# A cross-attention and MLP block on one Trainium2 core: in the last five of 32 attention units the ones product runs on the sum of the two key halves, under a newly planned order

## The chip, the cores and the metric

The kernel runs on one core of a Trainium2 chip. The core's engines are TensorE (PE, matrix products; PEld is its weight load), VectorE (DVE), ScalarE (ACT), GpSimd (POOL) and SyncE (SP), which here issues the DMA transfers. The engines run side by side and meet at semaphores. The metric is the time of one execution on the device in microseconds (us). The kernel before took 677.11, 676.02 and 676.46 us in three runs, median 676.46.

## The reference

One transformer block in fp32: layer norm, cross-attention with 16 heads, residual, layer norm, MLP with gelu, residual. There are 8 batches of 256 tokens, the width D is 512, the MLP's 2048, a head has 32 columns, and the context has 256 keys per batch. The mask is all ones.

```python
x = layer_norm(hidden_states, ln1_w, ln1_b)
q = (x @ q_w + q_b)...                       # to (B, 16 heads, 256, 32)
k = (encoder_hidden_states @ k_w + k_b)...
v = (encoder_hidden_states @ v_w + v_b)...
scores = jnp.einsum('bhqd,bhkd->bhqk', q, k) * scale
scores = jnp.where(mask, scores, mask_value)
attn = jax.nn.softmax(scores, axis=-1)
out = jnp.einsum('bhqk,bhkd->bhqd', attn, v)
hidden = out @ cproj_w + cproj_b + residual  # out as (B, 256, 512)
y = layer_norm(hidden, ln2_w, ln2_b)
y = jax.nn.gelu(y @ fc_w + fc_b, approximate=True)
return hidden + y @ proj_w + proj_b
```

## The kernel before, in words

The tokens are worked on in two groups of 1024 (g = 0 and 1, four batches each). Every large matrix product is done by a recursion with seven products instead of eight (`quad`, line 837): products P1 to P7 go to PSUM banks, and DVE, ACT or POOL add them up (operations named t1 to t3 and c11 to c22) and make the sums of the operands beforehand (`sums`, line 816; names such as x1t1 for sums of activations, and pw1s1 or pw1i2_4 for sums of weights). The MLP's two products, fc and pd, do this on two levels (`grown`, line 1146).

**Attention** is cut into 32 units, 16 for each group. A unit is named by three digits: group, head group (four heads) and batch; unit 123 is group 1, head group 2, batch 3. For each unit `scores` (line 991) and `attend` (line 1039) record these operations, named by kind and unit:

- `s` on PE: the scores of four heads, keys on the partitions, in two halves of 128 keys; eight matmuls in row shape.
- `ev` on ACT (eight): copies from PSUM to the two tiles `pr`, with the mask's bias.
- `mx` (two), `mt` on DVE, `mc` (three) on ACT, `fold` on DVE: the maxima over the keys for each query. Then `md` stores them to DRAM and `mm` loads them back on all partitions; both are issued by SP.
- `less` (two, on POOL or DVE): subtract the maxima. `exp` (two) on ACT.
- `av` on PE, in column shape: eight matmuls with a matrix of ones give the sums over the keys (four heads, two halves of the keys each, added up in PSUM), and eight with the values give the output. A matmul of fp32 shows as two records in the profile.
- `r` on DVE (maximum over equal rows with a transpose, reciprocal, transpose), and `att` on DVE (output times reciprocal).

The code knows a second kind of unit. A string of letters, one for each unit of a group in order of work, chooses it (line 502); all 32 are `p` before. For a unit with the letter `z`, `scores` also records two additions `ss` of 128x512 (one for each `pr` tile, on DVE or POOL) that add the two halves of the keys, and `attend` issues four matmuls with ones on that sum instead of eight on the halves:

```python
if ss:
    sums_ = [(lambda j=j: tile_of(av)[j * HD : (j + 1) * HD, 256:512], lambda: ones, lambda j=j: at(ss, j), True) for j in range(4)]
else:
    sums_ = [(lambda j=j: tile_of(av)[j * HD : (j + 1) * HD, 256:512], lambda: ones,
              lambda j=j, kc=kc: at(pt[j // 2], 2 * (j % 2) + kc), kc == 0) for kc in range(2) for j in range(4)]
```

The units of a group go in the order of `units_of` (line 1321); the last five of group 1 are 123, 111, 131, 113 and 133.

**The order is written out by hand.** The kernel first records all 2,927 operations (class `Order`, line 44), each with the buffers that it reads and writes. `run` (line 94) then reads a long string, `PROGRAM` (line 124), in which each operation stands once, and plays it back: `name:V`, `:A` or `:G` puts it on DVE, ACT or POOL, and a name without a letter goes to its usual engine. A second string, `PLACES`, gives each buffer its slot of SBUF (45 slots of 128x1024 and smaller ones) or its bank of PSUM (three for the projections, five for scores and outputs). So the order in which an engine runs its instructions is the order of the words, and an instruction that waits holds up all that stands behind it on its engine. All DMA is issued by SP in this order too, so a load that stands behind a store that waits is late with it.

Around unit 003, one of group 0's last, the words in `PROGRAM` (lines 186 to 196) run, on PE: s003, av001, v1_1_P7, three turns (transposes), av032, q1_0_P1, s023, v1_1_P4, a turn, v1_0_P4, s011, q1_1_P1, av021, s031, av003. The keys of unit 011 come from DRAM by the load ku011, which stands far ahead (line 164). Between fold003 and less003_0 DVE has pw1s3, pw1i6_3, less021, pw1i6_1, less021 again, att032, mx023 twice, mt023, pw1i6_4 and x1t1; pw1i7_1 stands between the two less003.

Behind the last unit of group 0, av033, PE has s120, o0_0_P2, o0_0_P1, o0_1_P1, s110 and o0_0_P6 (the o products are the attention's output projection). o0_0_P6 needs a0t2, a sum of attention outputs on DVE, and this needs r033, att033 and a copy on ACT, ab0_111. While units of group 1 go through their softmax, PE runs fc products of group 0.

Of the kernel before, what the change touches and what calls it, by code (L numbers as in the profile page):

```python
# [124 lines left out]
cq0_00_0 cq0_00_1 vw00 rows8 kw00 cq0_01_1 mk rows4 turn_c0_10 cq0_01_0 turn_c0_00 c0_10:V cq0_11_0 c0_00:A  # L125
cq0_11_1 rows6 small k0_0_P1 kw11 cq0_10_0 rows2 k0_1_P1 kw10 cq0_10_1 rows3 turn_c0_11 rows1 turn_c0_01 c0_11:A
turn_c0_21 fw0_00_0 c0_01:V turn_c0_31 vw11 c0_21:V v0_1_P1 c0_31:A rows5 c0t3:V kw01 xt0_0 v0_0_P1 kws1:G rows7
rows0 vw10 kws3:V turn_c0_20 fw0_10_0 mk~1 turn_c0_30 c0t1:V c0_20:A k0_1_P7 vw01 c0_30:A fw0_11_1 v0_0_t1:A
v0_1_t1:V kws2:G fw0_11_0 k0_0_P2 fw0_10_1 c0t2:V fw1_11_1 fw0_00_1 kws4:G cols k0_1_P2 cols~1 fw0_01_1 k0_1_t1:A
vws1:V xt0_2 k0_0_t1:A vws3:G xt0_7 k0_1_P6 k0_1_c11 xt0_3 xt0_1 c0t4:V fw1_10_1 k0_0_P6 xt0_5 vws2:V xt0_4 fw0s1:V  # L130
xt0_6 v0_1_P6 k0_0_t2:A fw0s2:V fcd0_5_False k0_1_t2:A qw00 vws4:V k0_1_P5 fw0_01_0 v0_1_t2:A stats_x0_10 fw0i6_3:G
xt1_2 fw0s3:V v0_1_P5 stats_x0_00 fw1i4_1:G stats_x0_11 fw0i5_3:G v0_0_P6 k0_0_c11 fw0i1_1:G stats_x0_21 aggr_x0_11
fw0i2_1:V aggr_x0_10 v0_1_P2 fw0i1_2:V fw0i7_1:V stats_x0_01 fw0i1_4:G aggr_x0_21 fw0i1_3:V k0_0_P5 aggr_x0_01
fw0i7_2:G aggr_x0_00 fcd0_1_True eps_x0_0 fw1_01_0 fw0i6_1:V pow_x0_0 v0_0_t2:V fw1_01_1 v0_0_P2 v0_1_t3:V
fw0i7_3:G k0_0_t3:A xt1_0 stats_x0_20 fw1_11_0 eps_x0_1 aggr_x0_20 eps_x0_2 fw0i5_1:V fcd0_7_False v0_0_P5 pow_x0_1
stats_x0_30 fw0i2_3:V stats_x0_31 fw0i6_2:G nb_x0_1 v0_1_P3 pow_x0_2 aggr_x0_30 norm_x0_11:A fw1_00_1 nb_x0_0
aggr_x0_31 fw0i5_2:G norm_x0_10:A qw10 nb_x0_2 qw11 fw1i2_1:V k0_1_t3:A k0_0_P3 fw0i2_2:V fw1_10_0 v0_0_t3:A
fw1i4_2:V k0_1_c22 fw0i2_4:G norm_x0_01:A fcd0_6_False eps_x0_3 fw1_00_0 fw1i4_3:V norm_x0_20:A k0_1_P3 pow_x0_3
v0_1_c11 norm_x0_00:A fw0i6_4:V v0_0_c11 fw0i7_4:G v0_0_P3 fw1i4_4:V fcd0_7_True fw0i5_4:G qw01 qws1:V fcd0_5_True
nb_x0_3 turn_x0_30 norm_x0_31:V fcd1_4_True k0_0_c12:A turn_x0_10 qws2:V turn_x0_00 x0_10:A fw1i2_3:V turn_x0_20  # L140
x0_00:A k0_1_P4 qws3:V v0_0_c12:A fw1i1_3:V x0_30:A fw1s1:V q0_0_P1 norm_x0_30:A fw0s4:V fcd1_5_False norm_x0_21:A
vd0_0_11 x0_20:A fw1s2:V turn_x0_21 fcd0_2_True k0_1_c12:A turn_x0_01 fcd0_6_True turn_x0_31 fw1i1_1:V kd0_0_11
turn_x0_11 fw1i5_1:V xt1_3 q0_1_P1 fw1s3:V v0_1_c12:A x0_21:A x0_01:V fw1i5_2:G x0_31:A q0_0_P2 fw1i1_2:G q0_0_t1:V
x0_11:A k0_1_c21 fw1i1_4:G q0_1_t1:A q0_1_P2 q0_0_c11 pw0_00_11 fw1i2_2:V x0t1:V fcd1_6_False kd0_1_12 s000
fcd1_7_False x0t2:V pw0_00_10 k0_0_P7 ev000_00 x0t3:V stats_x1_00 ev000_21 q0_0_P6 ev000_30 fw1i5_3:V ev000_31
aggr_x1_00 fw1s4:V q0_1_P6 q0_0_t2:A fw1i2_4:V x0t4:V ev000_10 fcd1_2_True q0_0_P5 fw1i5_4:V q0_1_t2:A stats_x1_10
fw1i7_3:G fcd1_5_True ev000_01 k0_0_c22 fcd0_3_False ev000_11 qws4:G stats_x1_11 fcd1_1_True q0_0_P7 q0_0_t3:A
fcd1_3_False mx000_0 fw1i3_1:G ev000_20 pw0_00_00 fw1i3_3:G ct1_4 k0_0_P4 q0_0_c22 ct1_1 fw0i3_3:G ct1_0 fw0i3_1:V
ct1_3 mx000_1 fw1i7_1:G q0_0_P4 fw0i4_3:G q0_1_P7 q0_0_c21 aggr_x1_10 q0_1_c11 k0_0_c21 q0_1_P5 aggr_x1_11
fw0i3_2:V mt000 fw0i3_4:V mc000_2 fw1i6_1:V mc000_3 fcd0_3_True mc000_1 fw1i3_2:V s020 q0_1_t3:A fw1i6_2:V fold000  # L150
fw1i3_4:G q0_1_c22 q0_0_P3 md000 fw1i6_3:G ev020_01 ev020_30 fcd1_3_True eps_x1_1 ev020_10 pow_x1_1 ct1_7 ev020_31
# [8 lines left out]
mc022_2 av000 ev010_01 ev010_21 less020_0:V ev010_10 ev010_30 ev010_00 k1_1_P1 exp020_1 c1t1:V mm002 ev010_20  # L160
fold022 ev010_11 c1t2:G exp020_0 k1_0_P1 mx010_0 md022 pw0_10_01 ev010_31 r000 q0_1_c12:A av020 k1_1_t1:A pw0i1_4:G
att000 k1_0_t1:A mx010_1 c1t3:G prd0_1_True mm022 s030 mt010 r020 mc010_2 mc010_3 mc010_1 k1_0_P6 ev030_21 fold010
ev030_11 pw0_01_11 less002_1:V ev030_00 md010 ev030_01 ev030_10 xt1_1 k1_1_P6 ev030_20 k1_0_t2:V pw0_10_10 ev030_30
less002_0:V ev030_31 pw0_01_00 exp002_1 pw0_10_00 k1_0_P5 less022_1:G mx030_0 ku011 exp002_0 pw0_01_10 mm010
# [318 lines left out]
def pool(n):  # L483
# [17 lines left out]
}  # L501
KINDS = ("pppppppppppppppp", "pppppppppppppppp")


SERVE = {
# [964 lines left out]
```

## Time and profile before

| | |
|---|---|
| median of three runs | 676.46 us (676.02 to 677.11) |
| profiled execution | 676.35 us |
| its span | 674.6 us |
| granted clock of TensorE, mean | 0.997 |
| instructions | 11,523 |
| busy: PE, PEld | 98%, 74% |
| busy: DVE, ACT, POOL | 86%, 50%, 56% |

The profile is of one execution. Its page has a line with the busy time of each engine, the span in 40 slices (each digit is the busy share in tenths; PEclk is the clock that TensorE was granted, in tenths), the chain of work that ended last, and groups of instructions (line, engine, operation, output<-inputs, shape, count, busy time and mean length in ns). The trace behind it answers with the waits (who waited for whom: us in total, times, longest), windows (busy time of each engine in a stretch) and a timeline (start, length, engine, line, operation). Names there are by kind of buffer: a row `av<-pr,ones` is a product with ones of some unit, and one finds which by the order of the words. Some buffers are shared: a name such as `vws` can stand for values of a unit.

### The profile page before, as it was taken

The page shows a single profiled execution, that of the slowest core. Times are in us where ns is not written, and L with a number is a line of the kernel's source. Part 1 is how long each engine was busy: PE and PEld are TensorE (multiplying, and loading weights), DVE is VectorE, ACT ScalarE, POOL GpSimd, SP SyncE. Part 2 cuts the span into 40 slices and gives each one's busy share as a digit, 9 for nine tenths or more (in the row PEclk, how much of TensorE's full clock was granted, in tenths as well). Part 3 has the DMA queues.
Part 4 walks back from the last instruction along what each step waited for, and adds up shares of the span by engine and source line. Part 5 has one row for each costly group of instructions (what it writes and reads, how often), then busy time and mean ns, then how long its engine had stood idle before and what let it go on. Part 6 is the DMA issues. An engine that isn't in the chain of part 4 may idle for free.

```text
span 674.6 us, 11523 instructions
## 1 busy us (share of the span) xinstructions
PE 663.8 (98%) x4001; PEld 498.3 (74%) x4001; DVE 578.3 (86%) x969; ACT 340.1 (50%) x699; POOL 379.1 (56%) x340
## 2 busy tenths in 40 slices
PE   9999999999899999999999999999999999999997
PEld 7674564478544676777687888888888888888886
DVE  2889889999999999999889999998489877896874
ACT  1246488768999979976764872001040221930000
POOL 1552556575578999977945743310636247518542
PEclk9999999999989999999999999999999999999999
DMA  8989888987957635445552646997999586842686
GB/s 264 329 273 337 306 286 257 295 258 211 307 164 241 210 113 203 157 142 170 174 190 95 220 130 167 267 245 250 165 243 237 133 243 149 232 144 57 192 166 118
DMA packets 173034, 140.65 MB, mean 209 GB/s; under 512 B 83712, under 2 KB 133424, under 8 KB 172976
## 3 DMA queue, kind: packets, MB, share of 16 engines
q1 hardware_dynamic: 172976, 139.92, 70.5%
q8 instruction: 32, 0.52, 0.3%
q14 instruction: 26, 0.21, 0.1%
HBM read 102.00 MB, written 37.88 MB: 207 GB/s over the span
## 4 chain that ended last, share of the span: by engine, by line
PE 92%; DVE 4%; DMA 3%; ACT 1%; issue 0%; SPq 0%; POOL 0%; DVEq 0%
PE fc_X L641 14%; PE pd_X L641 14%; PE fc_W L641 7%; PE pd_W L641 7%; PE av L641 6%; PE s L641 4%; PE k_X L641 4%; PE v_X L641 4%; PE q_X L641 4%; PE o_X L641 4%; PE pd_Y L641 4%; PE fc_Y L641 3%; PE k_W L641 2%; PE v_W L641 2%; PE o_W L641 2%; PE q_W L641 2%
## 5 line engine op out<-in xcount | busy, mean ns | idle before, releaser
L621 ACT ACTIVATE pr<-s,cols 128x256 f32<-128x256 f32 x256 | 103.1, 480 | 30.5 <-PE s L641 24.5
L1029 POOL TENSOR_TENSOR pr<-pr,mm 128x512 f32<-128x512 f32 x74 | 98.1, 1353 | 28.8 <-ACT pr L621 9.5
L1004 DVE TRANSPOSE_TENSOR_REDUCE mx<-pr 128x32 f32<-128x1024 f32 x64 | 77.6, 1222 | 1.9 <-ACT pr L621 1.8
L1209 ACT ACTIVATE h<-h,cols 128x256 f32<-128x256 f32 x128 | 54.6, 496 | 48.4 <-DVE h L632 45.5
L1032 ACT ACTIVATE pr<-pr 128x1024 f32<-128x1024 f32 x64 | 66.9, 1066 | 3.8 <-POOL pr L1029 2.9
L632 DVE TENSOR_TENSOR h<-fc_X,h 128x512 f32<-128x512 f32 x80 | 53.0, 678 | 10.0 <-PE fc_X L641 8.3
L641 PE MATMUL av<-pr,ones 128*32 128x256 f32 x512 | 35.1, 392 | 3.5 <-ACT pr L621 3.3
L632 DVE TENSOR_TENSOR h<-fc_W,h 128x512 f32<-128x512 f32 x48 | 32.1, 680 | 5.1 <-PE fc_W L641 4.9
L1024 DVE TENSOR_TENSOR pr<-pr,mm 128x1024 f32<-128x1024 f32 x27 | 34.8, 1310 | 0.9 <-DMA mm<-md 0.9
L1011 ACT COPY mx<-mx 32x64 f32<-32x64 f32 x96 | 23.3, 243 | 16.6 <-DVE mx L1008 13.4
L630 POOL TENSOR_TENSOR z1i<-z1t,z1i 128x512 f32<-128x512 f32 x12 | 16.8, 1420 | 26.0 <-issue 16.3
L641 PEld LDWEIGHTS av<-pr,ones 128*32 128x32 f32 x512 | 14.4, 110 | 21.8 <-issue 5.9
L632 POOL TENSOR_TENSOR h<-h,fl 128x512 f32<-128x512 f32 x16 | 21.4, 1350 | 8.6 <-DVE h L632 7.5
L613 ACT ACTIVATE e<-pd_X,cols 128x256 f32<-128x256 f32 x4 | 1.9, 468 | 44.1 <-PE pd_X L641 31.9
L641 PE MATMUL fc_W<-y1i,fl 128*128 128x256 f32 x92 | 22.8, 379 | 0.0
L641 PE MATMUL pd_X<-z1i,pl 128*128 128x256 f32 x96 | 22.0, 379 | 0.0
L796 POOL TENSOR_TENSOR rs_y<-rs_y,neg_half 128x2 f32<-128x2 f32 x8 | 8.2, 1034 | 23.4 <-DVE rs_y L793 22.8
L1012 DVE TENSOR_REDUCE mx<-mx 32x32 f32<-32x256 f32 x32 | 18.5, 580 | 2.4 <-ACT mx L1011 2.2
L641 PE MATMUL pd_W<-z1i,pl 128*128 128x256 f32 x88 | 20.5, 379 | 0.0
L641 PEld LDWEIGHTS pd_X<-z1i,pl 128*128 128x128 f32 x96 | 18.2, 190 | 2.5
L641 PEld LDWEIGHTS fc_W<-y1i,fl 128*128 128x128 f32 x92 | 17.5, 190 | 2.4
L641 PE MATMUL pd_X<-z0i,pl 128*128 128x256 f32 x80 | 19.0, 380 | 0.0
(593 smaller groups left out, 1836.3 us busy)
## 6 DMA issues: line engine op xcount, KB each, us to landing
mm<-md SPq DMA_DIRECT2D x32, 512.0 KB, 4.9
pl<-prd SPq DMA_DIRECT2D x52, 256.0 KB, 4.4
fl<-fcd SPq DMA_DIRECT2D x41, 256.0 KB, 4.1
fl<-prd SPq DMA_DIRECT2D x18, 256.0 KB, 4.6
fw<-in_L_xattn_fc_w_dram SPq DMA_DIRECT2D x16, 256.0 KB, 5.3
pw<-in_L_xattn_proj_w_dram SPq DMA_DIRECT2D x32, 128.0 KB, 3.1
hid<-in_x_dram SPq DMA_DIRECT2D x8, 512.0 KB, 3.6
hd<-hid SPq DMA_DIRECT2D x8, 512.0 KB
```

What stands on the lines that cost most here:

```text
L621: lambda e: nc.scalar.activation(to(), of_(), AF.Identity, bias=bias(), scale=1.0))
L630: nc.gpsimd.tensor_tensor(to()[:, ts(k, 512)], in0()[:, ts(k, 512)], in1()[:, ts(k, 512)], op)
L632: E[e].tensor_tensor(to(), in0(), in1(), op)
L641: nc.tensor.matmul(o(), l(), r(), start=first, stop=True, skip_group_check=True)
L796: lambda e, rs=rs: nc.gpsimd.tensor_tensor(tile_of(rs)[:, 2:4], tile_of(rs)[:, 0:2], neg_half[:, 0:2], ALU.pow), lock=True)
L1004: T.op(f"mx{u}_{h}", [("DVE", 1.126)], [(pr[h], None)], [(mx, [h])], lambda e, h=h: nc.vector.tensor_reduce(tile_of(mx)[:, 0:64].rearrange ...
L1011: lambda e, a=a: nc.scalar.copy(tile_of(mx)[0:32, 64 + 64 * a : 128 + 64 * a], tile_of(mx)[32 * a : 32 * a + 32, 64:128]))
L1012: T.op(f"fold{u}", [("DVE", 0.38)], [(mx, [2, 3, 4, 5])], [(mx, [6])], lambda e: nc.vector.tensor_reduce(tile_of(mx)[0:32, 320:352], tile_ ...
L1024: nc.vector.tensor_tensor(p_, p_, m_[:, :, None, :].to_broadcast([P, 2, 2, S]), ALU.subtract)
L1029: E[e].tensor_tensor(p_, p_, at(M, j)[:, None, :].to_broadcast([P, 2, S]), ALU.subtract)
L1032: lambda e, h=h: nc.scalar.activation(tile_of(pr[h]), tile_of(pr[h]), AF.Exp), table="exp")
L1209: lambda e, f=f, b=b, c=c: nc.scalar.activation(at(h[f][b], c), at(h[f][b], c), AF.Gelu_apprx_tanh, bias=col(c_fcb + f * 4 + c), scale=1.0 ...
```

## The change

Five units become `z`, and the two strings are planned anew for it. The one line outside them:

```diff
-KINDS = ("pppppppppppppppp", "pppppppppppppppp")
+KINDS = ("pppppppppppppppp", "pppppppppppzzzzz")
```

The diff has 703 lines, nearly all of `PROGRAM` and `PLACES`: the stages follow one another as before, but nearly every line has operations in other places, some on another engine, and most buffers in other slots. There are ten operations more, the additions `ss`:

```diff
+fc016_c22 exp123_1 fc006_c21 less123_0:G att121 s131 mm111 r103 fl017_0 fc002_P6 fl002_1 fc012_c22 ev131_21
+ss123_1:G ev131_31 fl005_0 ev131_30 fc016_P4 fc002_t2 fl003_0 exp123_0 fc012_P4 fc016_c21 ev131_11 ss123_0:G
+ev131_01 fc002_P5 fc012_c21 ev131_20 ev131_00 mx131_1 fc002_P7 less111_1:G ev131_10 av123 att103 fc002_t3 mx131_0
...
```

Seven of them are on POOL (both of units 123, 111 and 131, and ss133_0), three on DVE (both of 113, and ss133_1). By the two orders:

| | before | after |
|---|---|---|
| operations | 2,927 | 2,937 |
| matmuls | 2,085 | 2,065 |
| operations on DVE, in all | 902 | 929 |
| of these ahead of s003; ahead of s133 | 229; 473 | 233; 481 |
| operations on POOL, in all | 253 | 234 |
| exp or gelu tables that ACT loads, by its order | 8 | 10 |
| changes of PE between full, row and column shapes | 98 | 100 |
| fc products between s and av: 123, 111, 131, 113, 133 | 27, 24, 31, 27, 45 | 28, 25, 33, 36, 45 |
| av of other units there, 111 | 3 | 4 |
| o products there, 133 | 0 | 2 |

Around unit 003 the order (left out words are those of other engines or stages):

```diff
-... v1_1_P3 ... fold021 s003 ... av001 ... v1_1_P7 ... av032 ... q1_0_P1 ... s023 fold003 ... md003 v1_1_P4
-... v1_0_P4 ... mm003 ... s011 ... q1_1_P1 ... av021 mt023 ... x1t1:V ... less003_0:V s031
-... pw1i7_1:V less003_1:V ... exp003_0 ... exp003_1 ... av003
+... s003 ... av001 ... v1_1_P3 ... v1_1_P7 ... av032 ... s023 ... v1_0_P4 ... fold003 ... md003 ... v1_1_P4 ... ku011
+... mm003 ... s011 ... q1_0_P1 ... q1_1_P1 ... less003_0:V ... less003_1:V ... s031
+exp003_0 x1t1:V ... av021 exp003_1 ... av003
```

So one more v product, v1_1_P3, stands between s003 and av003; x1t1 and one of the pw1i pieces stand behind less003 instead of ahead of it; and ku011 stands behind md003. Behind av033 PE has o0_0_P1, s110, o0_0_P2 and o0_0_P6. At the start the loads of the context and of the weights are in another order, and the first products are of v instead of k; the fourth of the large loads is the first weight in both. At the end the same pieces come in another order. Behind av133, the last av, POOL has 19 operations fewer than before and DVE 18 more.

More of the change, by code (lines that the diff above doesn't have):

```diff
@@ L124 @@
 PROGRAM = """
[L125 to L139, printed above, removed]
@@ L160 @@
[L160 to L164, printed above, removed]
@@ L190 @@
-att001 mc003_3 v1_1_c22 x1_11:A pw1i2_2:G r032 mc003_2 mc003_1 pw1i2_4:G ab0_000 s023 fold003 pw1s3:V md003 v1_1_P4
-ev023_20 ku033 ev023_31 pw1i6_3:V ev023_21 prd1_7_False less021_0:V ev023_11 ev023_10 turn_x1_01 ev023_30 pw1i6_1:V
-v1_0_P4 ev023_00 mm003 less021_1:V ev023_01 prd1_6_False x1_01:A ow10 att032 exp021_1 pw1s4:G s011 vd0_1_21
-v1_0_c21 ku013 mx023_1 exp021_0 vd0_1_12 q1_1_P1 prd1_5_False ev011_30 mx023_0 ev011_00 pw1i6_2:G ev011_20 ev011_11
-av021 mt023 ev011_21 pw1i6_4:V ev011_10 x1t1:V prd1_6_True ev011_01 fl012_2 ev011_31 q1_0_t1:A less003_0:V s031
@@ L350 @@
[L350 to L352 removed]
+cq0_00_0 cq0_00_1 cq0_10_1 vw00 cq0_11_1 cq0_11_0 cq0_10_0 mk turn_c0_10 cq0_01_0 turn_c0_00 c0_10:A cq0_01_1
+c0_00:V kw00 vw01 small v0_1_P1 vw11 v0_0_P1 rows1 v0_1_t1:A rows7 fw0_00_1 turn_c0_20 turn_c0_30 vw10 c0_20:A
@@ new lines @@
+fw0_01_0 v0_1_c11 qw10 kws2:V cols k0_1_P2 v0_0_t3:A fcd0_7_False stats_x0_31 qw01 fw0s1:V v0_0_P3 fw0i5_1:V cols~1
+fw0i5_2:G k0_1_t1:A fw0s2:V k0_0_P2 stats_x0_21 kws4:G stats_x0_00 k0_1_P7 aggr_x0_21 fw0i6_1:G stats_x0_10
+k0_0_t1:V fw0i1_4:G k0_1_P6 fw0i6_2:V fw1_11_0 stats_x0_30 fw0i2_3:G vd0_0_11 aggr_x0_10 stats_x0_20 fw0i6_4:G
+fw1_10_0 aggr_x0_11 k0_0_P6 stats_x0_01 fw0i2_2:G k0_1_t2:A fw1_11_1 aggr_x0_20 aggr_x0_00 aggr_x0_01 eps_x0_1
+qws3:V fcd0_5_False pow_x0_1 qw11 k0_1_P5 k0_0_t2:A fw0i5_3:V fcd0_1_True eps_x0_0 v0_1_t3:A nb_x0_1 fw0i2_4:V
@@ new lines @@
+ev003_30 md021 pw1i1_3:G ev003_31 prd1_4_True ev003_21 v1_1_P3 pw1i1_4:G r001 ev003_20 ev003_10 prd1_1_True
+exp032_1 pw1s3:V ku031 v1_1_P7 ev003_01 mm021 ev003_11 pw1s1:V pw1_01_10 ev003_00 exp032_0 pw1_01_00 turn_x1_31
+pw1_01_11 v1_1_c22 pw1s2:G turn_x1_21 att001 turn_x1_11 x1_21:A mx003_1 av032 x1_31:A mx003_0 x1_11:A pw1i6_1:G
+ab0_000 s023 mt003 pw1i6_2:G r032 mc003_1 mc003_2 pw1i7_3:G mc003_3 v1_0_P4 ev023_01 fold003 pw1i6_4:G ev023_10
+att032 ev023_11 md003 less021_0:V ev023_30 pw1_01_01 ev023_20 v1_1_P4 ev023_31 ku011 pw1i6_3:V ev023_00 less021_1:V
@@ new lines @@
+ev023_21 mm003 exp021_0 prd1_6_False turn_x1_01 vd0_1_21 pw1i2_1:V v1_1_c12:A pw1i2_3:V prd1_6_True exp021_1
+mx023_0 pw1i2_2:G s011 pw1s4:G x1_01:A mx023_1 q1_0_P1 ev011_00 ev011_11 v1_0_c21 ev011_20 ev011_21 mt023 ev011_30
+q1_1_P1 pw1i2_4:V mc023_2 less003_0:V ev011_01 prd1_2_True ev011_10 ku033 ev011_31 less003_1:V mc023_1 vu011 s031
+exp003_0 x1t1:V mc023_3 av021 exp003_1 fold023 ev031_20 x1t2:G ev031_21 mx011_1 md023 ev031_31 av003 q1_1_t1:A
+vu013 mx011_0 ev031_01 ev031_00 pw1i5_3:G mt011 mm023 q1_1_P6 r021 mc011_2 ev031_11 x1t3:G ev031_10 att021 ev031_30
@@ new lines @@
+rc001=2 ku011=3 vu011=10 s011_0=0 s011_1=4 s011_2=3 s011_3=2 pr011_0=56 pr011_1=18 mx011=1 mm011=2 av021=4 r021=6
+rc021=4 ku031=8 vu031=9 s031_0=2 s031_1=1 s031_2=3 s031_3=0 pr031_0=58 pr031_1=68 mx031=2 mm031=82 av003=3 r003=7
+rc003=7 ku013=13 vu013=5 s013_0=4 s013_1=2 s013_2=0 s013_3=1 pr013_0=22 pr013_1=32 mx013=0 mm013=2 av023=0 r023=3
+rc023=4 ku033=3 vu033=6 s033_0=0 s033_1=1 s033_2=2 s033_3=3 pr033_0=30 pr033_1=6 mx033=1 mm033=26 av011=1 r011=1
+rc011=3 av031=1 r031=10 rc031=9 av013=3 r013=4 rc013=8 av033=4 r033=8 rc033=6 ct1_0=46 ct1_1=76 ct1_2=77 ct1_3=47
@@ L468 @@
+ot1=70 ps_o01=4 ps_o10=0
 """
```

631 lines of the change are left out of this document (316 added, 315 removed).

## The prediction

> **What bounds the kernel now.** I read the page's busy line and slices first, then whom TensorE (PE) waited for, then the windows and the chain around its longest wait.
>
> ```profile
> span 674.6 us, 11523 instructions
> ...
> PE 663.8 (98%) x4001; PEld 498.3 (74%) x4001; DVE 578.3 (86%) x969; ACT 340.1 (50%) x699; POOL 379.1 (56%) x340
> ...
> PE   9999999999899999999999999999999999999997
> ...
> DVE  2889889999999999999889999998489877896874
> ...
> PEclk9999999999989999999999999999999999999999
> ```
>
> PE is busy in 98% of the span, so time is won by fewer PE instructions or from the 10.8 us in which PE idles. PE has one slice of 8 away from the end, PEclk has one just behind it. The profiled execution took 676.35 us, 0.1 below the median of 676.46; the sum starts from 676.35, of which 674.6 is the span.
>
> PE's longest waits (total, times, longest), then windows (length, busy of PE, PEld, DVE, ACT, POOL with counts, granted clock, DMA share, GB/s; the last holds the five units), then the chain (start, length):
>
> ```profile
> PE av L641 <- ACT pr L621: 3.3, 1, 3.3
> PE ps_y L728 <- DVE att L632: 1.1, 1, 1.1
> ...
> PE o_X L641 <- DVE a0t L632: 0.5, 1, 0.5
> ```
>
> ```profile
> 180.00:195.00 15.00, 11.72 (x107) 5.56 (x106) 14.48 (x25) 13.45 (x34) 10.46 (x11) 0.89 0.75 249
> ...
> 45.00:195.00 150.00, 146.51 (x983) 86.24 (x982) 140.75 (x239) 111.34 (x236) 83.20 (x83) 0.99 0.85 278
> ...
> 318.00:381.00 63.00, 62.80 (x435) 48.96 (x435) 56.85 (x96) 43.11 (x77) 45.30 (x41) 1.00 0.53 171
> ```
>
> ```profile
> 162.43 1.08 PE s L641 x16
> ...
> 173.62 1.92 PE v_W L641 x8
> ...
> 175.98 1.73 PE v_W L641 x8
> ...
> 182.56 1.17 PE s L641 x16
> 183.73 0.45 ACT pr L621
> 184.19 1.94 ACT pr L1032 x2
> ...
> 186.91 3.37 PE av L641 x32
> ```
>
> The av at 186.91 is unit 003's; by the written order its scores are the s at 162.43. PE has 21.3 us of work between (162.4 to 183.7), the softmax takes 24.5, so PE stands 3.2. Then the clock falls: this av takes 3.37 us. What one takes otherwise (and an fc product, for later):
>
> ```profile
> 302.21 1.86 PE av L641 x32
> ...
> 307.07 0.86 PE fc_Y L641 x4
> ```
>
> So 3.3 + 1.5 = 4.8 us go there. The clock dropped at no other wait: PEclk has no other 8, so the wait of 1.1 did not cost it.
>
> **The change, part by part.**
>
> *Products with ones.* One av is two rows of the timeline:
>
> ```profile
> 180.63 1.07 PE L641 MATMUL av<-pr,ones 128*32 128x256 f32 x16
> 181.51 1.05 PE L641 MATMUL av<-pr,vws 128*32 128x256 f32 x16
> ```
>
> From start to start the ones take 0.88 us for 16 records, eight for each half of the keys. One half goes: 0.44 in each of five units, −2.2, all on PE's path. The planned order changes between row, column and full array shapes 100 times instead of 98; an s took 1.17 instead of 1.08 above, 0.1 for an unlucky neighbour: +0.2.
>
> *Ten additions*, 128x512, seven on POOL and three on VectorE (DVE). Nearest rows, same size:
>
> ```profile
> L632 DVE TENSOR_TENSOR h<-fc_X,h 128x512 f32<-128x512 f32 x80 | 53.0, 678 | 10.0 <-PE fc_X L641 8.3 <-POOL h L632 1.2 <-DMA mm<-md 0.2
> ...
> L632 POOL TENSOR_TENSOR h<-h,fl 128x512 f32<-128x512 f32 x16 | 21.4, 1350 | 8.6 <-DVE h L632 7.5 <-DVE fl L632 1.1
> ```
>
> Each stands between the unit's exponentials and its av. The tightest unit before is 111 (its last exponential, its av; then the table load ahead of unit 131's):
>
> ```profile
> 333.03 1.05 ACT L1032 ACTIVATE pr<-pr 128x1024 f32<-128x1024 f32 x1
> ...
> 335.36 1.07 PE L641 MATMUL av<-pr,ones 128*32 128x256 f32 x16
> ...
> 352.74 1.28 ACT L1032 ACT_TABLE_LOAD   x1
> ```
>
> It has 335.36 − 334.08 = 1.28 us of slack; POOL's add takes 1.35. But the new order gives each of the first four more PE work between s and av: 123 one fc product, 111 one fc product and one av, 131 two, 113 nine; 133 gets two o products. With 0.86 more, slack is 2.1 at least and covers one add. If the cover goes, av is late by what is over: 0 to 0.6 where both adds stand in line on POOL (2 x 1.35 − 2.1). I take 0. By program order ACT loads tables ten times instead of eight (1.28 each); ACT is 50% busy, and the same slack hides them: 0.
>
> *The new order around unit 003.* Between s003 and av003 stands one more v product (v1_1_P3), 1.73 by the chain: −1.7 of the gap. On DVE x1t1 and one pw1i piece are moved behind less003:
>
> ```profile
> 173.28 0.32 SPq L601 DMA_DIRECT2D md<-mx  x1
> 176.10 0.33 SPq L595 DMA_DIRECT2D mm<-md  x1
> ...
> 181.22 1.22 DVE L632 TENSOR_TENSOR x1t<-x,x 128x1024 f32<-128x1024 f32 x1
> 182.35 1.22 DVE L1024 TENSOR_TENSOR pr<-pr,mm 128x1024 f32<-128x1024 f32 x1
> 183.49 0.42 DVE L632 TENSOR_TENSOR pw1i<-pw1s 128x256 f32<-128x256 f32 x1
> ```
>
> ```profile
> DMA to landing us min/median/max: 3.7/4.9/6.0
> ```
>
> (The last is of tile mm.) The maxima of unit 003, stored at 173.28 and issued at 176.10 land by 181.0, so the chain can come 182.35 − 181.0 = 1.35 earlier, plus 0.3 for the piece between: −1.7 at most. Against it, DVE has four more operations up to s003 (233 for 229 by the two orders), moved there from other engines or later places; at some 0.6 each (140.75 us over 239 in the window from 45) +2.4 if DVE, 94% busy, makes up nothing, 0 if it makes up all. Together −1.7 to +0.7; I take the middle, −0.5. The gap becomes 3.3 − 1.7 − 0.5 = 1.1.
>
> At 1.1, like the waits that kept the clock, the half clock goes: −1.5. The other end is 0 (a rival).
>
> *SP's queue.* ku011, the keys of unit 011, is moved behind md003, which waits for fold003; s011 stands 14.4 us of PE work behind s003. ku's landing:
>
> ```profile
> DMA to landing us min/median/max: 2.4/2.8/5.5
> ```
>
> md003 was issued 10.9 us after the s of its unit (173.28 − 162.4); with 2.8 for ku, s011 comes due at 13.7, with 5.5 at 16.4: a wait of 0 to 2.0, middle 1.0. It stands within unit 003's stretch, so it only uses up the remaining gap of 1.1: +0 (up to +2.0 where the gap is gone).
>
> *Unit 033 to o0_0_P6.* The order leaves 4.9 us of PE work (two o products at 1.92, as v_W above, one s of 1.08) behind av033 instead of 7.9 (three and two). The chain there, by the order: the reciprocal (227.51 to 228.66), att, a copy on ACT, then a0t (timeline):
>
> ```profile
> 227.51 0.40 DVE L1055 TRANSPOSE_TENSOR_REDUCE rc<-av 128x8 f32<-128x256 f32 x1
> ...
> 228.66 0.42 DVE L632 TENSOR_TENSOR att<-av,r 128x256 f32<-128x256 f32 x1
> 229.00 2.36 DVE L1004 TRANSPOSE_TENSOR_REDUCE mx<-pr 128x32 f32<-128x1024 f32 x2
> 229.48 0.72 ACT L621 ACTIVATE att<-att,cols 128x512 f32<-128x512 f32 x1
> ...
> 232.00 3.50 POOL L630 TENSOR_TENSOR a0t<-att,att 128x512 f32<-128x512 f32 x2
> 232.14 2.24 DVE L632 TENSOR_TENSOR a0t<-att,a0t 128x1024 f32<-128x1024 f32 x1
> ```
>
> 1.15 + 0.42 + 0.72 + 2.24 = 4.5, or 6.9 with the 2.4 of two maxima in DVE's queue. Wait 0 to 2.0, middle 1.0, against 0.5 now: +0.5.
>
> *At nothing.* The loads of the start change places, but the first product still needs the fourth large one: 0. Behind av133 POOL has 19 operations fewer and DVE 18 more; they lie in the last 18 slices, where DVE goes down to 4, 6 and 7, and find idle time: 0. The tail has the same pieces in another order: 0. Elsewhere neighbours change places; the waits that this may make are in the rivals.
>
> Sum: 676.35 − 2.2 + 0.2 − 1.7 − 0.5 − 1.5 + 0 + 0.5 = 671.2 (rounded up from 671.15). Its own range: 668.9 (gap gone whole, −3.3 instead of −2.2 for both its terms; no wait at P6, −0.5; no shape cost, and ku in time) to 673.4 (chain +0.7 instead of −0.5, P6 +1.5).
>
> *A rule against the change.* The a0t rows show POOL and DVE holding each other up: 2.24 us for what x1t, of the same size, takes in 1.22. Were DVE held up by that 1.0 at each of the seven POOL additions, it would be 7 us, against the 6.15 (63.00 − 56.85) that DVE idles in the window of the five units: 0.9 over, a sum of 672.1 instead of 671.2, and more where the holds stand badly (third rival). The Trainium skill, SBUF — State Buffer, "Who interferes with whom", says that a DVE instruction with two SBUF inputs contends with a GpSimd one that reads SBUF. By that rule every such meeting costs; the trace agrees in the a0t rows.
>
> **The rivals.**
>
> *Gap and half clock stay.* Another late softmax, or ku011 at 5.5, keeps PE standing over 3 us: 676.35 − 2.2 + 0.2 = 674.4, up to 675.9 with P6 at 1.5. For: DVE's 94%. Against: the added product is sure.
>
> *VectorE becomes the bound: slower.* Up to s133 DVE has eight more operations (481 for 473), 4.8 us at 0.6. Place: its queue from 45 us on, where it idles 9 of 150 us and 0.5 of 15 behind unit 003. It decides once the lag is over slack such as the 1.28 us between exponentials and av; then each further lag stands on PE: 676.35 − 2.2 + 0.2 + 4.8 = 679.2 with the gap as now, 676.8 if half is made up. For: three additions and the moved pieces are DVE's. Against: DVE idles 6.15 us in the window of the five units, more than the lag.
>
> *The additions delay their av: the change doesn't do what it says.* Three units with POOL adds late by 0.6 each, plus DVE held up by about 1.0 per POOL add and idle for less (7 − 6.15, up to 3 if badly placed): 671.2 + 1.8 + 0.9 to 3 = 673.9 to 676.0; with the gap as now as well, 3.2 more. For: the a0t row. Against: the longer leads.
>
> **How the numbers follow.** A measurement tells about 0.2%, 1.35 us: 675.1 to 677.8 is no change. My forecast has 0.42, all faster, since two of its terms (products with ones, the added product) are sure in sign. Gap stays: 0.18 (0.11 faster, 0.07 same). VectorE: 0.25 (0.05 same, 0.20 slower), so high because nearly every line of the order moved. Additions late: 0.15 (0.04 faster, 0.04 same, 0.07 slower, where it meets the gap). Faster 0.57, same 0.16, slower 0.27. The range goes from 669.0 to VectorE's 679.2; the likeliest case alone has 668.9 to 673.4.
>
> **What would show it.** Ones in units 123 to 133 with half the records and 0.44 us each. The wait of av on ACT's pr down from 3.3 to about 1, the clock 1.00 in 180 to 195, no av of 3.37. Additions of 1.35 (POOL) and 0.68 (DVE) that no av of PE waits for. o_X waiting for a0t about 1. Wrong it would be by a new wait of over 2 us of PE on DVE, on pr, or on a load (ku, fl), or by a second dip of the clock.

## The result

The changed kernel took 677.9 us (median of 14 runs, 676.4 to 679.1), the kernel before 676.52 (14 runs beside it, 674.63 to 677.35): a ratio of 1.0025, 95% interval 1.0017 to 1.0033. The change made the kernel slower by 1.4 us, where the prediction had 671.2 and faster. The time lies inside the range, on the wrong side of no change.

The profiled execution of the changed kernel took 677.88 us, span 676.1 (before: 676.35 and 674.6). Its page, and TensorE's waits (total, times, longest). Line numbers are two higher than before, since the order's text is two lines longer.

```profile
span 676.1 us, 11396 instructions
...
PE 661.8 (98%) x3961; PEld 496.9 (73%) x3961; DVE 596.6 (88%) x996; ACT 342.9 (51%) x703; POOL 348.5 (52%) x310
...
PE   8999999999999998999999999999999999998997
...
PEclk9999999999999999999999999999999999999999
```

```profile
PE av L643 <- DVE att L634: 1.7, 1, 1.7
PE pd_Y L643 <- DMA pl<-prd: 1.4, 1, 1.4
PE first L655 <- DVE warm L650: 1.0, 1, 1.0
PE v_X L643 <- DMA vw<-in_L_xattn_v_w_dram: 0.8, 1, 0.8
PE pd_X L643 <- DVE po L855: 0.7, 1, 0.7
PE ps_y L730 <- DVE y L768: 0.7, 1, 0.7
PE pd_W L643 <- DMA xn_y<-in_L_xattn_proj_w_dram: 0.7, 1, 0.7
```

The one wait of 3.3 us and the dip of the clock are gone, and PE is busy 2.0 us less. But PE stands 676.1 − 661.8 = 14.3 us instead of 10.8: many waits of about a microsecond have come in its place, two of them for loads of the last stage. In windows (length, busy of PE, PEld, DVE, ACT, POOL, then clock, DMA share, GB/s), first the kernel after, then before:

```profile
180.00:195.00 15.00, 14.32 (x128) 6.84 (x128) 14.65 (x25) 14.24 (x35) 10.98 (x13) 1.00 0.58 191
240.00:280.00 40.00, 37.27 (x370) 26.76 (x373) 38.48 (x82) 34.44 (x67) 36.03 (x31) 1.00 0.56 168
...
318.00:381.00 63.00, 62.88 (x412) 49.74 (x411) 56.47 (x95) 47.45 (x84) 51.21 (x42) 1.00 0.51 158
...
580.00:640.00 60.00, 57.98 (x268) 50.46 (x267) 54.22 (x66) 13.91 (x35) 3.48 (x4) 1.00 0.63 137
```

```profile
240.00:280.00 40.00, 38.62 (x370) 28.57 (x372) 38.53 (x83) 37.50 (x72) 37.13 (x34) 1.00 0.51 169
...
580.00:640.00 60.00, 60.00 (x279) 52.72 (x278) 49.23 (x61) 16.23 (x41) 30.08 (x21) 1.00 0.48 142
```

Around unit 003 (180 to 195) PE stands 0.7 us instead of the 3.3 of before; in the window of the five units it stands 0.1. It loses in 240 to 280 (2.7 for 1.4) and above all in 580 to 640, where before it did not stand at all. There POOL's work fell from 30.1 to 3.5 us and VectorE's rose from 49.2 to 54.2.

The av of unit 003 and, further on, one of a `z` unit (unit 111) in the kernel after:

```profile
185.67 1.07 PE L643 MATMUL av<-pr,ones 128*32 128x256 f32 x16 [0.40 <-ACT pr L623]
...
337.00 0.64 PE L643 MATMUL av<-ss,ones 128*32 128x256 f32 x8
337.45 1.05 PE L643 MATMUL av<-pr,v 128*32 128x256 f32 x16
```

Unit 003's stand is 0.4. The product with ones of the `z` unit has half the records and takes 0.45 us from start to start, as forecast.

To place the losses I also went by starts: for each operation, its start less the usual lengths of all that stands ahead of it on PE (such as 1.73 for a v product, 1.92 for a q product, 0.86 for an fc product, and 0.43 less for the av of a `z` unit), which tells how late PE is. Lateness after minus lateness before:

| at | late by, more than before, us |
|---|---|
| start of s003 (161.6 us after, 162.4 before) | +1.0 |
| start of s013, behind av003 (189.4, 190.2) | −2.7 |
| start of s112 (243.8, 244.5) | −0.8 |
| start of fc011_P1 (274.5, 272.4) | +1.2 |
| start of s133 (338.4, 337.2) | +0.3 |
| start of pd12_P1 (608.6, 615.7) | +0.3 |
| end of PE's last operation (672.4, 670.8) | +3.7 |

The work itself is 2.15 less; 3.7 − 2.15 is the 1.5 by which the span grew. So the new order won 3.7 us at unit 003, lost 1.0 ahead of it, gave back 3.9 between 190 and 275, won 0.9 up to unit 133, and lost 3.4 in the last stage.

### The profile page after: what moved, and what is told of

Its sections match the earlier page's. It is cut to its first block, busy times and chain, and to the rows that moved or that the text cites. A ratio compares the mean times of both kernels' runs of the same rounds, so it can differ in the third digit from the quotient of the medians.

```text
span 676.1 us, 11396 instructions
## 1 busy us (share of the span) xinstructions
PE 661.8 (98%) x3961; PEld 496.9 (73%) x3961; DVE 596.6 (88%) x996; ACT 342.9 (51%) x703; POOL 348.5 (52%) x310
## 4 chain that ended last, share of the span: by engine, by line
PE 84%; DVE 5%; ACT 4%; DMA 3%; issue 2%; SPq 1%; POOL 0%; DVEq 0%; ACTq 0%
PE fc_X L643 15%; PE pd_X L643 13%; PE fc_W L643 7%; PE pd_W L643 6%; PE av L643 6%; PE o_X L643 4%; PE k_X L643 4%; PE v_X L643 4%; PE s L643 4%; PE fc_Y L643 4%; PE pd_Y L643 3%; PE q_X L643 3%; PE k_W L643 2%; ACT pr L623 2%; PE q_W L643 1%
## 5 line engine op out<-in xcount | busy, mean ns | idle before, releaser
L1031 POOL TENSOR_TENSOR pr<-pr,mm 128x512 f32<-128x512 f32 x78 | 101.4, 1329 | 19.9 <-DMA mm<-md 18.5
L634 DVE TENSOR_TENSOR h<-fc_X,h 128x512 f32<-128x512 f32 x80 | 52.4, 679 | 11.0 <-PE fc_X L643 10.8
L634 POOL TENSOR_TENSOR po<-po,e 128x256 f32<-128x256 f32 x6 | 6.8, 1137 | 88.1 <-PE pd_W L643 56.5
L1026 DVE TENSOR_TENSOR pr<-pr,mm 128x1024 f32<-128x1024 f32 x25 | 31.3, 1264 | 1.1 <-DMA mm<-md 1.1
L643 PE MATMUL av<-pr,ones 128*32 128x256 f32 x432 | 28.8, 384 | 2.8 <-DVE att L634 1.7
L643 PE MATMUL pd_W<-z0i,pl 128*128 128x256 f32 x88 | 20.3, 379 | 0.0
L643 PE MATMUL fc_X<-y1i,fl 128*128 128x256 f32 x80 | 20.0, 381 | 0.0
L634 DVE TENSOR_TENSOR h<-fc_Y,h 128x512 f32<-128x512 f32 x24 | 16.2, 680 | 3.1 <-PE fc_Y L643 2.9
L634 POOL TENSOR_TENSOR tq<-tq,rq 128x512 f32<-128x512 f32 x8 | 10.2, 1275 | 16.1 <-DVE tq L1312 8.7
L643 PEld LDWEIGHTS pd_W<-z0i,pl 128*128 128x128 f32 x88 | 16.7, 190 | 2.3
L610 ACT COPY h<-fc_X 128x512 f32<-128x512 f32 x12 | 7.0, 592 | 21.4 <-PE fc_X L643 21.4
```

Of the source, the lines that this page charges most:

```text
L610: (nc.scalar.copy if e == "ACT" else nc.vector.tensor_copy)(to(), of_())
L634: E[e].tensor_tensor(to(), in0(), in1(), op)
L643: nc.tensor.matmul(o(), l(), r(), start=first, stop=True, skip_group_check=True)
L1026: nc.vector.tensor_tensor(p_, p_, m_[:, :, None, :].to_broadcast([P, 2, 2, S]), ALU.subtract)
L1031: E[e].tensor_tensor(p_, p_, at(M, j)[:, None, :].to_broadcast([P, 2, S]), ALU.subtract)
```

## The experiments

Each was compared with the kernel before on the same chip in the same job; that one took 675.9 to 676.1 in all of them, and 676.5 beside the kernel after. So a difference between two kernels of different jobs is also given by their ratios to the kernel before.

**What the halving is worth.** `e1_order_only` keeps the new order and places, drops the ten additions and takes the ones on both halves in all units. `e10_loads_moved_without_sums` does the same to a kernel that comes below, where the last stage's loads are not in the way (`e6_loads_moved_up`, 676.3).

```diff
-KINDS = ("pppppppppppppppp", "pppppppppppzzzzz")
+KINDS = ("pppppppppppppppp", "pppppppppppppppp")
-... ss123_1:G ... ss123_0:G ... ss111_1:G ... ss133_1:V ...
```

> The new order and places kept, but the ten additions left out and all 32 units with the product with ones on both halves. Theory (the halving is worth 0.44 us in each of five units, and the new order gave it back elsewhere): 677.9 + 2.2 = 680.1, within 0.6. Rival (the additions cost what they save, by holding POOL, VectorE or av): 677.9 or less.

> The kernel of e6_loads_moved_up without the ten additions, all 32 units with the product with ones on both halves; to have the halving by itself where the late loads are no longer in the way. Theory (0.44 us in each of five units, nothing lost on the additions): 676.3 + 2.2 = 678.5. Rival (the additions cost what they save where nothing else hides it): 676.3 or less; and if the 3.4 that e1_order_only lost belongs to the halving in full: 679.7.

e1 took 681.31 (ratio 1.0075, interval 1.0061 to 1.009), 3.4 more than the kernel after, by the ratios too. On PE the last operation ends 2.0 later than after (674.4 for 672.4). The other 1.4 lie behind PE's end: SP issues the sixteen stores ahead of the last two until 673.9 instead of 670.2, and no run explains why. e10 took 678.34 (1.0036, 1.0022 to 1.0049), 2.0 more than e6, or 2.2 by the ratios. The halving is worth what was forecast, some 2 us, and the additions take none of it away in this order. The trace of the kernel after says the same: of the tile of the sums, the operations and who waited for them.

```profile
L634 POOL TENSOR_TENSOR ss<-pr x7: 1272/1277/1711, 322.9 to 371.6; 128x512 f32<-128x512 f32 x7
L634 DVE TENSOR_TENSOR ss<-pr x3: 676/692/693, 361.3 to 382.6; 128x512 f32<-128x512 f32 x3
...
who waited for it (us, times):
busy tenths in 40 slices 0000000000000000000715300000000000000000
```

The list of those who waited is empty. So the 1.4 us are lost by the order, not by the sums.

**The additions without the order.** `e2_sums_in_old_order` and `e11_sums_placed_in_old_order` put eight of the additions into the order of before (four of the five units, all but 113). e2 has six on POOL and two on VectorE, e11 two on POOL and six on VectorE.

```diff
-KINDS = ("pppppppppppppppp", "pppppppppppppppp")
+KINDS = ("pppppppppppppppp", "pppppppppppzzzpz")
-SLOTS = {"Q": (45, 1024), ...
+SLOTS = {"Q": (46, 1024), ...
+... exp123_0 ss123_0:G ... exp123_1 ss123_1:V ... (e2: each right behind its exponential)
+... att103 ss123_0:V ... fc002_c22 ss123_1:V ...  (e11: where the exponential is done)
```

> The kernel before, its order kept, with the additions and the single product with ones in four of the five units (123, 111, 131 and 133; one more buffer slot of 128x1024 holds the sums, six additions on POOL, two on VectorE, each right behind its exponential). Theory: 676.5 - 4 x 0.44 = 674.8, within 0.5. Rival (the additions cost what they save): 676.5 or more.

> As e2_sums_in_old_order (the kernel before, four units with additions), but the additions are put where their exponential is already done by the trace of the kernel before, six on VectorE and two on POOL, so that no list waits for ScalarE at them. Theory (e2 lost 7.5 us because an addition at the head of VectorE's or POOL's list waited for its exponential and held the evacuations of fc behind it): most of that goes, 675 to 677. Rival (VectorE and POOL have no room for the additions there, wherever they stand): 680 or more.

e2 took 683.64 (1.0117, 1.0097 to 1.0137), e11 680.45 (1.0062, 1.005 to 1.0075). My theory failed in e2 and mostly in e11. PE's waits in e2, and two additions, one on each engine:

```profile
PE fc_X L633 <- DVE h L624: 3.5, 3, 1.8
...
PE fc_W L633 <- DVE h L624: 2.1, 1, 2.1
```

```profile
326.06 1.65 DVE L624 TENSOR_TENSOR ss<-pr 128x512 f32<-128x512 f32 x1 [1.55 <-ACT pr L1024]
...
358.97 3.66 POOL L624 TENSOR_TENSOR ss<-pr 128x512 f32<-128x512 f32 x2 [3.11 <-ACT pr L1024]
```

VectorE stood 1.55 us at the head of its list for an exponential, and then the addition took 1.65 instead of 0.68, while POOL was subtracting maxima. The additions of fc that free PE's banks stood behind it. POOL stood 3.11 us ahead of two of its additions. In e11 VectorE no longer waits at an addition (POOL still does, 2.75 and 0.30 us at its two), and PE still waits 3.7 us for VectorE's h (2.4 for fc_X, 1.3 for fc_W). So the additions, free in the new order, are not free at these two sets of places; VectorE was busy 56.85 of the 63 us before. e11 moved four more additions to VectorE as well, so it does not part the place from the engine, and no run of this order has all of them on POOL at places where the exponential is done.

**The last stage.** In the kernel after, SP's issues, VectorE's sums and PE's two waits (timeline; in brackets what ended the idle time ahead of the row):

```profile
591.12 0.48 SPq L597 DMA_DIRECT2D fl<-prd  x1
601.20 0.32 SPq L597 DMA_DIRECT2D pl<-prd  x1
...
599.90 1.22 DVE L634 TENSOR_TENSOR z1t<-h,h 128x1024 f32<-128x1024 f32 x1
...
611.15 1.97 PE L643 MATMUL pd_W<-z1i,xn_y 128*128 128x256 f32 x8 [0.67 <-DMA xn_y<-in_L_xattn_proj_w_dram]
...
616.20 1.97 PE L643 MATMUL pd_Y<-z1t,pl 128*128 128x256 f32 x8 [1.36 <-DMA pl<-prd]
```

SP issues nothing from 591.6 to 601.2. The load it stands at, pl17_2, goes to the slot of a tile that the sum z1t1_2 reads last, and this sum, the row at 599.90, ends at 601.1: it is the twelfth that VectorE runs since 586. In the kernel before it is the third, ahead of nine of these, and pl17_2 stands far earlier in SP's list and goes to another slot. The weight loads behind pl17_2 are late with it.

It looks as if VectorE were late because POOL's sums had come to it. But of the twelve only z1i7_2 was POOL's before, and up to this point VectorE had no more to do than before (first the kernel before, then after):

```profile
580.00:604.00 24.00, 24.00 (x113) 21.01 (x111) 23.26 (x28) 15.36 (x39) 5.99 (x4) 1.00 0.51 152
```

```profile
580.00:604.00 24.00, 24.00 (x113) 21.13 (x112) 22.28 (x25) 13.04 (x33) 0.77 (x1) 1.00 0.25 66
```

So it is the place of this sum in VectorE's list, with the slot and the place of the load, that differs. Three kernels test this: `e5_sum_moved_up` lets that sum run earlier, `e6_loads_moved_up` lets two loads pass, `e3_late_sums_on_pool` relieves VectorE.

```diff
 e5: -... z1t2_0:V gelu1_202 z1t1_2:V ...   +... pd11_c11 z1t1_2:V ...
 e6: -... pl17_2 ... pl11_4 ... pl16_2 ...   +... pl11_4 pl16_2 pl17_2 ...
 e3: -z1t1_3:V ... z1i5_1:V ...             +z1t1_3:G ... z1i5_1:G ...   (twelve sums)
```

> The kernel after with one sum, z1t1_2, moved up on VectorE's list, from behind z1t2_0 to behind pd11_c11; nothing else. Theory (SP's queue stood from 591.6 to 601.2 because this sum held the slot that the load pl17_2 goes to): the sum ends about 597.7 instead of 601.1, SP goes on then, TensorE's waits of 0.7 and 1.4 us at pd11_P4 and pd16_P2 go: 677.9 - 2.1 = 675.8. Rival (SP or the transfers are late for another reason, the DMA engines being full there): the waits stay, 677.9.

> The kernel after with the loads pl11_4 and pl16_2 moved ahead of pl17_2 in SP's queue; VectorE's list as it is. Theory (they are late only because they stand behind pl17_2): the same two waits go, 675.8. Rival (the transfers are late by themselves, or pl17_2 and its followers then come late): 677.9 or more.

> The kernel after with twelve sums of the last stage (z1t1_3, z1t2_3, z1t3_1, z1t3_3, z1t4_0, z1t4_1, z1t4_2, z1i1_4, z1i2_1, z1i3_1, z1i5_1, z1i5_3) on POOL instead of VectorE, nothing else. Theory (VectorE, with 18 operations more there, held a buffer slot until 601.1 us, so SP's queue stood from 591.6 to 601.2 and two loads came late for TensorE): the waits of 0.7 and 1.4 us go, 675.8, and 674.6 if the third (0.9) goes too. Rival (the loads are late by their place in SP's queue or by the transfers themselves): 677.9. If POOL with 2.5 us each is too slow for them: over 678.

e5 took 676.04 (1.0004, 0.9993 to 1.0015) and e6 676.3 (1.0004, 0.9994 to 1.0015): 1.9 and 1.6 less than the kernel after (1.4 each by the ratios), and in both the two waits are gone from PE's list. One move of a sum, or of two loads, brings back what these two waits cost. In e5 SP goes on earlier, and PE does not stand between 580 and 640 (last row), though VectorE has as much work there as in the kernel after and POOL only 6.0 us:

```profile
590.86 0.48 SPq L587 DMA_DIRECT2D fl<-prd  x1
598.66 0.32 SPq L587 DMA_DIRECT2D pl<-prd  x1
...
580.00:640.00 60.00, 60.00 (x280) 52.89 (x279) 54.98 (x69) 13.65 (x34) 5.97 (x6) 1.00 0.61 143
```

e3 went the other way: 684.24 (1.0116, 1.01 to 1.0133). On POOL each of its twelve sums is two of 128x512. Its sums on the two engines, and SP:

```profile
589.75 7.90 POOL L622 TENSOR_TENSOR z1t<-h,h 128x512 f32<-128x512 f32 x4
...
589.17 3.92 DVE L624 TENSOR_TENSOR z1t<-h,h 128x1024 f32<-128x1024 f32 x2
...
600.87 2.28 DVE L624 TENSOR_TENSOR z1i<-z1t,z1t 128x1024 f32<-128x1024 f32 x1
...
592.78 0.48 SPq L587 DMA_DIRECT2D fl<-prd  x1
607.66 0.32 SPq L587 DMA_DIRECT2D pl<-prd  x1
```

Run together, a sum of 128x1024 takes VectorE 1.96 to 2.28 us instead of 1.22, and half of one takes POOL 1.97 instead of 1.27. The sums end later, z1t1_2 at 607.6, SP stands until 607.7, and PE waits 3.0 us for the load where it waited 0.7. It also waits 2.1 at an earlier product, and the 1.4 is gone. So e3 tells nothing of what less work on VectorE would be worth, but it moved the end of this sum, SP's issue and the wait together, in the direction that the explanation says.

**The place at unit 003.** The prediction read the stand as a softmax that lacked PE work ahead of it. `e4_gap_closed_in_old_order` gives the kernel before just the two moves that the prediction counted.

```diff
-v1_1_P3 ... s003 ... av001 ... x1t1:V ... less003_0:V ... pw1i7_1:V less003_1:V
+s003 ... av001 v1_1_P3 ... less003_0:V ... less003_1:V x1t1:V pw1i7_1:V
```

> The kernel before with v1_1_P3 moved from ahead of s003 to behind av001, and x1t1 and one pw1i piece moved behind the two less003; nothing else, no halving. Theory (the gap at av003 was one softmax late against TensorE's work): 1.7 us of work more and a chain up to 1.7 us earlier close it to 0 to 1 us and the half clock goes: 671.7 to 673.4. Rival (the half clock is no consequence of the wait, or the wait comes back at the next unit): 674.8 or more.

It took 678.12 (1.0028, 1.0016 to 1.0039), and its profile has the stand as before:

```profile
187.40 1.07 PE L632 MATMUL av<-pr,ones 128*32 128x256 f32 x16 [3.31 <-ACT pr L612]
```

This wait names the copies of scores (L612 here, L621 in the kernel before), not the exponentials. By the places, av003 shares a bank with the scores of unit 031, which ScalarE's copies ev031_21 and ev031_20 free; and ScalarE's list in the kernel before runs

```profile
183.72 0.47 ACT L621 ACTIVATE pr<-s,cols 128x256 f32<-128x256 f32 x1
184.09 2.04 ACT L1032 ACTIVATE pr<-pr 128x1024 f32<-128x1024 f32 x2
186.04 2.64 ACT L621 ACTIVATE pr<-s,cols 128x256 f32<-128x256 f32 x7
```

so: one copy of unit 031, both exponentials of 003, then those two copies. The copies wait for s031, the operation just ahead of av003 on PE, and the exponentials stand behind one of them. So in this order work on PE ahead of s031 doesn't fill the stand. (e4's other eleven runs were 0.6 to 3.8 above its profiled one, which has two new waits, 0.8 in v_W and 0.8 in two av; why it is slower is open.) `e9_exponentials_first` changes ScalarE's list and makes e4's moves on VectorE too, `e8_av021_behind_s031` changes PE's order, each in the kernel before:

```diff
 e9: -s031 mc023_1 mc023_2 mc023_3 ... ev031_01 exp003_0 ... exp003_1 ... ev031_21 ... ev031_20
     +exp003_0 exp003_1 s031 ev031_21 ev031_20 ... mc023_1 mc023_2 mc023_3 ev031_01
 e8: -av021 ... s031 ... av003     +s031 av021 ... av003
```

> The kernel before with ScalarE's list around unit 003 changed: both exponentials ahead of mc023 and of all copies of unit 031, then ev031_21 and ev031_20 (which free av003's bank), and x1t1 and one pw1i piece behind the two less003 on VectorE; TensorE's order as it is. Theory (ScalarE's list between s031 and av003 makes the stand): less003 ends 183.5, the exponentials 184.9, the two copies 185.6, so av003 starts at 185.6 instead of 186.9: a stand of 2.0 instead of 3.3; 674.8, or 673.3 if the half clock goes at 2.0. Rival (as at unit 023 and av110, what is put back, here mc023 by 1.3 us, makes TensorE stand later): 676 or more.

> The kernel before with av021 moved behind s031 on TensorE, as the kernel after has it; nothing else. Theory (ScalarE, not the softmax chain of unit 003, sets this place: s031 needs the banks that ScalarE's copies of s011 free at 182.3, and av003 needs a bank that ScalarE frees with ev031_20 behind both exponentials): TensorE stands 1.6 us at s031 and 1.5 at av003 instead of 3.3 at once, the same in sum; 676.1, or 674.6 where the half clock goes with the long stand. Rival (av003 only lacks work ahead of it): the stand goes down to 1.4 and the half clock goes, 672.7.

In e9 av003 starts at 185.57, forecast 185.6, and the stand is 1.9:

```profile
182.74 2.06 ACT L1023 ACTIVATE pr<-pr 128x1024 f32<-128x1024 f32 x2
184.63 0.89 ACT L612 ACTIVATE pr<-s,cols 128x256 f32<-128x256 f32 x2
...
185.57 1.07 PE L632 MATMUL av<-pr,ones 128*32 128x256 f32 x16 [1.88 <-ACT pr L612]
188.31 0.70 PE L632 MATMUL s<-xt,ku 32*128 32x256 f32 x4 [0.80 <-ACT pr L612]
189.74 1.39 PE L632 MATMUL s<-xt,ku 32*128 32x256 f32 x12 [0.74 <-DVE att L623]
```

That shows ScalarE's list as a cause, together with VectorE's. The second subtraction of unit 003 (less003_1) in the kernel before, and both in e4:

```profile
183.82 1.22 DVE L1024 TENSOR_TENSOR pr<-pr,mm 128x1024 f32<-128x1024 f32 x1
```

```profile
181.65 2.35 DVE L1015 TENSOR_TENSOR pr<-pr,mm 128x1024 f32<-128x1024 f32 x2
```

In e4 both had ended at 184.0, and the stand was the same. In the kernel before the second ends at 185.0, when the second exponential starts, so ScalarE's list alone, which no run changes by itself, could hardly have made the exponentials earlier. But the copies that were put back made the next scores wait 0.8, VectorE another 0.74, the clock dipped behind them, and the kernel took 676.88 (1.0019, 1.0009 to 1.003): nothing won. In e8 PE stood 1.6 us at s031, as forecast, but then 3.3 at av003 again, where I had 1.5, because the exponentials still stood behind ev031_01; 676.94 (1.001, 0.9999 to 1.0021). The kernel after has all of it in one: VectorE's moves, exponentials ahead of the copies and av021 behind s031, and there the stand is 0.4. What each gives there is not shown.

**What was given back.** `e7_after_mended` takes four waits out of the kernel after, `e12_maximum_behind_att122` takes e6 and moves one maximum that VectorE ran ahead of att122, for whose bank av110 waits (the 1.7 at the top of the list after).

```diff
 e7:  e5 and e6, and  +z1t4_3:V pd13_t3 z1i4_2:V   +r122 att122
 e12: e6, and         -mx132_0 ... mt132 ... att122   +att122 ... norm_y0_11:V mx132_0 mt132
```

> The kernel after with both moves (z1t1_2 up on VectorE, pl11_4 and pl16_2 up on SP), with pd13_t3 ahead of z1i4_2 on VectorE, and att122 right behind r122. Theory (new waits, not the halving, ate the gain): the three waits of the last stage (0.7, 1.4, 0.9) and 0.6 of the wait at av110 go: 677.9 - 3.6 = 674.3, below the kernel before at 676.1. Rival (a wait that is taken away comes back at the next late operation): 676 to 678.

> The kernel of e6_loads_moved_up with one maximum of unit 132 (mx132_0, 1.2 us on VectorE) and what follows from it (mt132, two mc132) moved from ahead of att122 to behind it; nothing else. Theory (the stand of 1.8 us at av110, where the new order gave back what it had won at unit 003, is VectorE's list being late: av110 waits for the bank that att122 frees): att122 ends 1.2 us earlier, the stand goes to about 0.6, and the layer norm behind it comes 1.2 earlier too, so the wait doesn't come back there: 676.3 - 1.2 = 675.1. Rival (another of the late operations takes its place, as in e7): 676 or more.

e7 took 676.49 (1.0013, 1.0001 to 1.0025), no better than e5 or e6 alone; e12 675.88 (0.9998, 0.9986 to 1.001). In e12 the wait at av110 is smaller, and a new one stands two operations later, at a turn:

```profile
PE ps_y L720 <- DVE att L624: 1.7, 1, 1.7
...
PE av L633 <- DVE att L624: 1.1, 1, 1.1
```

In the kernel after PE waits 1.7 + 0.3 + 0.7 = 2.7 us at av110 and the turns behind it, in e12 1.1 + 1.7 = 2.8. The rival was right in e7. In e12 its waits came back as it says, and the time lies just under its 676. Between 240 and 280 VectorE has 38.5 us of work in 40, and what is taken from one of its operations is missed at the next. No kernel here beats the one before by more than the measurement tells.

## Why the prediction was wrong

The step that failed is *At nothing*: the new order outside unit 003 was put at 0 and cost 7.4 us.

*At nothing.* "The tail has the same pieces in another order: 0" cost 3.4 us. 2.0 of them are the two waits for loads that e5 and e6 take away, 0.7 is a wait of pd_X for po, and the rest stands in no list. The path ran through SP: a sum that stood twelfth in VectorE's list instead of third held a slot too long and stopped the queue of loads. "Behind av133 POOL has 19 operations fewer and DVE 18 more; they ... find idle time: 0" is not what failed, as far as the runs show: VectorE still idles 5.8 us of 60 between 580 and 640, and in e5 as much work on it goes without a stand. "Elsewhere neighbours change places; the waits that this may make are in the rivals" cost 1.0 ahead of unit 003 and 3.9 between 190 and 275, and won 0.9 up to unit 133. So 1.0 + 3.9 − 0.9 + 3.4 = 7.4 stand against the 2.15 of the halving and the 3.7 won at unit 003. Of the 3.9 the profile names the waits at av110 and the turns behind it (2.7 us instead of 1.4); where the rest arose is open.

*Products with ones, −2.2*: right (2.15 in PE's work; 2.0 to 2.2 by e10 against e6). *The shapes, +0.2*: no run tests it.

*The ten additions, 0*: right in this order, but for less reason than I gave. I took leads of PE as the cover; in e2 and e11 PE waits mostly for VectorE's other operations behind the additions, so the places in the lists count too.

*v1_1_P3, −1.7*: wrong. e4 has that product moved and the same stand of 3.3. I had the rows for it: the wait names L621, the copies, and I quoted them at 183.73 and read them as part of the softmax. *The chain, −0.5*: by itself it gives nothing (e4), with ScalarE's list changed the stand falls by 1.4 (e9). At this place the prediction's terms (−1.7, −0.5 and the clock's −1.5) come to −3.7, and 3.7 was won there. That is luck: it came by ScalarE's list and av021, which I had not weighed.

*The half clock, −1.5*: right, it went. All 14 runs of the kernel after have a mean clock of 0.998 to 1.000. What it may be worth shows in the kernel before itself: of 35 runs of it in one job, 22 at 0.996 or 0.997 have a median of 676.1, nine at 0.994 one of 676.4 and four at 1.000 one of 674.8.

*ku011, 0*: right within its range (s011 starts 0.3 late). *P6, +0.5*: too high; no wait is left there in the profiled execution, and e10 has one of 0.3, where the kernel before had 0.5. (The range begins at 669.0, 0.1 above the 668.9 of its own likeliest case; nothing hangs on it.)

*The sign of being wrong*, a new wait of over 2 us or a second dip, did not come either: the loss is spread over many waits of up to 1.7.

*The rivals.* The second, VectorE as the bound, gave 676.8 to 679.2, and 677.9 came. That it did is partly luck: this rival's sum kept the gap and counted eight operations more up to s133, but the gap went, and in the window of the five units PE stands 0.1 us. What it had right is that PE waits for VectorE's list, at av110. The third was wrong in the kernel after (nobody waits for a sum).

*The rule.* The Trainium skill, SBUF — State Buffer, "Who interferes with whom", is borne out by e3 and e2, as by the a0t rows: with both engines adding out of SBUF, 1.22 becomes up to 2.28 and POOL's 1.27 becomes 1.97. It decided nothing in the five units, where POOL's additions took 1.28 in the median and VectorE's 0.69.

## What to carry to other kernels

In a planned order, price the stages that the edit doesn't name. Busy shares and counts of operations were no guide here: for each load of such a stage, find the operation that frees its slot and see whether it now stands later in its engine's list. A wait's row names the operation that freed something; look up which buffer that is before filling the gap with work, for here work ahead of the releasing chain's start did not fill it. And a store or load that waits for a slot holds every load behind it, so one late operation of an engine off the path can still stop PE through the DMA queue.

## What the runs showed of the hardware

The clock did not go by the length of a stand alone. The kernel before has a stand of 3.3 us with half clock behind it in its profiled execution; of 35 other runs of it, 31 have a mean clock of 0.994 to 0.997 and four one of 1.000, as if without a dip. In e4's profiled execution a stand of 3.31 had none (clock 1.00 in 180 to 195). In e9 stands of 1.9, 0.8 and 0.7 with scores and one av between them had a dip behind them too (window from 191 to 195):

```profile
180.00:195.00 15.00, 11.69 (x110) 5.57 (x109) 14.48 (x24) 13.96 (x35) 10.50 (x13) 1.00 0.77 260
```

```profile
191.00:195.00 4.00, 4.00 (x8) 1.80 (x7) 3.69 (x8) 3.65 (x9) 3.92 (x6) 0.64 0.26 81
```

The first row is e4's, the second e9's. The Trainium skill, TensorE: Matmul & The Clock Gate, Part 1, says that the clock is halved after an idle window of about 3.4 us and that the windows run freely. Windows that run freely agree with runs of one kernel that differ; that a single stand must fill the 3.4 does not agree with the 3.3 of the kernel before, and still less with e9, where the longest was 1.9.
